# A gated cross-attention and mixture-of-experts kernel: where a bias is added to the residual rows, and in which order the last expert tile is multiplied

## The chip, the cores and the metric

The kernel runs on one core of a Trainium2 chip. Its engines are the TensorE (PE in the profile, its weight loads PEld), the VectorE (DVE), the ScalarE (ACT), the GpSimd (POOL) and the SyncE (SP), which only issues DMAs here. Each engine works through its own queue of instructions in a fixed order and meets the others at semaphores. The metric is device time in microseconds (us); lower is better. The kernel before took 1280.68 us (median of 3 runs, 1278.86 to 1280.71).

## What is computed

Two blocks, each with an attention part and a feed-forward part that is added to the residual x (4 batches of 512 rows, 512 columns, float32). The change lies wholly in the last part of the second block, a mixture of 8 experts (inner width 352) with 2 experts per row and a shared expert (inner width 704) for every row:

```python
probs = softmax(x @ router_w.T)
topk_w, topk_idx = top_k(probs, 2); topk_w /= sum(topk_w)
for each expert e:                       # weight ce per row, 0 for most rows
    acc += ce * (silu(x @ gate_w[e]) * (x @ up_w[e]) @ down_w[e])
shared = silu(x @ s_gate_w + s_gate_b) * (x @ s_up_w + s_up_b) @ s_down_w + s_down_b
x_out = x + tanh(g_ffn[1]) * (acc + shared)      # here "x @" means layernorm(x) @
```

## The kernel before

The 2048 rows are 16 tiles of 128 rows, 4 tiles to a batch. The residual lives in SBUF as `x_sb`, one 128x512 block per tile. The last part of the kernel is written as five stages.

**Norm and shared expert, first half (L1160 to L1303).** `normed(b)` takes the layer-norm statistics of the batch (DVE, L121/L122; then two small POOL instructions `ve` L124 and `rstd` L126) and, tile by tile, writes the normed rows to `vx` (DVE, L130), transposes them on the PE (`tpd`, L1170) and copies them to `xnT_d` (ACT, L1173). `shared_hidden(0, b, ...)` multiplies batch b by gate and up columns of the shared expert: three chunks, each 16 matmuls into one PSUM buffer `gu` (L1219), then silu with bias on ACT (`sg`, L1207) and the product on DVE (`hd`, L1208). The norm tiles of batch b+1 are laid between the chunks of batch b. `shared_down(b)` multiplies by the down weights (`od`, L1255) and a DVE instruction (L1262) adds the result to `x_sb`; it runs one batch behind. PSUM has three such large buffers (`big`), which `gu`, `tpd`, `gue` and `oe` share, and two smaller ones (`acc`).

**Routing (L1307 to L1408).** A chain of small DVE instructions picks the two experts per row, counts them (PE, L1346 and L1354), and works out for every row the slot in a list sorted by expert. It ends with the row numbers `goi` (L1404).

**Scattering (L1410 to L1420).** 32 indirect DMAs issued by POOL (L1413) write the normed rows to the list `slots` in DRAM.

**Bias and shared expert, second half (L1428 to L1439).** The shared expert's down bias, already multiplied by the gate (`sdb`, made by L1126 and L1127), is added to all 16 tiles of `x_sb` by 16 POOL instructions in L1429. Then come the remaining gate and up columns, the last `shared_down` and two calls of `shared_down_two`, which also write `x_sb` to the output.

**Experts (L1442 to L1537).** The list has up to 39 tiles of 128 slots (`MT`); 36 of them are worked through here, the last three stand in a branch on the number used and are not entered with these inputs. For each tile j: `slot_rows` loads the rows (`xr`) and, where the expert changes, its weights, and turns the rows on the PE (`tpe`); `slot_hidden` makes 16 matmuls `gue` (gate and up in turn for each quarter of the depth), silu (`sge`, ACT) and the product (`he`, DVE); `slot_turn` turns it (`tph_e` on PE, `hT` on DVE); `slot_down` makes 6 matmuls `oe`, copies them (`ye`, ACT), and POOL issues an indirect DMA (L1499) that adds the 128 rows to the output. These adding DMAs are chained by hand: each waits until the one before has landed. The loop in `slot_tiles` is staggered: tile j's `slot_hidden` comes before tile j-1's turn and down.

The order of each engine's queue is made at compile time. Program order is the priority, but an instruction whose inputs are expected ready earlier is put ahead of earlier-written ones that are expected to wait. So the queue is not the text: the 4 bias adds of batch 3 run at 716 us, long before the routing that is written ahead of them, while those of batches 0 to 2 follow the L1262 additions to the same rows, at 759, 792 and 827 us. `tc.keep_in_program_order(ins)` pins an instruction behind the one written before it on the same engine.

Of the kernel before, what the change touches and what calls it, by code (L numbers as in the profile page):

```python
# [10 lines left out]
F32 = mybir.dt.float32  # L11
# [4 lines left out]
AF = mybir.ActivationFunctionType  # L16
ALU = mybir.AluOpType
# [3 lines left out]
P = 128  # L21
B, S, D = 4, 512, 512
NT = B * S // P
TB = S // P
DC = D // P
# [4 lines left out]
E, I = 8, 352  # L30

ICH = ((0, 128), (128, 128), (256, 96))
# [16 lines left out]
def flamingo_kernel(  # L49
# [22 lines left out]
    nc = tc.nc  # L72
# [6 lines left out]
    def big(name):  # L79
        return ps_big.tile([P, 2, 512], F32, tag="big", name=name)  # L80
# [5 lines left out]
    ident = const.tile([P, P], F32, name="ident")  # L86
# [7 lines left out]
    x_sb = const.tile([P, NT, D], F32, name="x_sb")  # L94
# [20 lines left out]
    def layer_norm_stats(b, tag, add=nc.vector):  # L115

        t0 = b * TB
        mv = small.tile([P, TB, 2], F32, tag="mv", name=f"mv_{tag}_{t0}")
        for i in range(TB):
            st = small.tile([P, 6], F32, tag="st", name=f"st_{tag}_{t0 + i}")  # L120
            nc.vector.bn_stats(st, x_sb[:, t0 + i, :])  # L121
            nc.vector.bn_aggr(mv[:, i, :], st)  # L122
        ve = small.tile([P, TB], F32, tag="ve", name=f"ve_{tag}_{t0}")
        add.tensor_scalar_add(ve, mv[:, :, 1], LN_EPS)  # L124
        rstd = small.tile([P, TB], F32, tag="rstd", name=f"rstd_{tag}_{t0}")
        nc.gpsimd.tensor_tensor(rstd, ve, mhalf, ALU.pow)  # L126
        return mv, rstd
# [104 lines left out]
    state = {"pend": None}  # L232
# [227 lines left out]
    def given(t):  # L460
        b, i = divmod(t, TB)
        return [(lambda cols=WHOLE, g=g: project(b, i, g, cols)) for g in range(NG)]
# [18 lines left out]
    for n in range(last_n + 1):  # L481
# [12 lines left out]
        elif n >= 7:  # L494
            stand_sums(behind, n, 1, n - 3)
            o = given(n - 7)
# [620 lines left out]
    fpool = ctx.enter_context(tc.tile_pool(name="fpool", bufs=2))  # L1117
# [7 lines left out]
    sdb = dpool.tile([P, D], F32, name="sdb")  # L1125
# [34 lines left out]
    def normed(b):  # L1160

        state["d"] = layer_norm_stats(b, "d", nc.gpsimd)

        def one_tile(i):
            t = b * TB + i
            v = vx[:, t, :D]
            layer_norm(v, t, i, *state["d"])
            tp = big(f"tpd_{t}")
            for dc in range(DC):
                nc.tensor.transpose(  # L1170
                    tp[:, 0, dc * P : (dc + 1) * P], v[:, dc * P : (dc + 1) * P], ident
                )
            nc.scalar.copy(  # L1173
                xnT[:, :, t * P : (t + 1) * P], tp[:, 0, :].rearrange("p (c q) -> p c q", q=P)
            )

        return [lambda i=i: one_tile(i) for i in range(TB)]
# [34 lines left out]
    def shared_hidden(n, b, h, chunks, between=()):  # L1212
        gw, uw, _ = shared_w[n]
        between = list(between)
        for c in range(chunks):
            gu = big(f"gu_{n}_{b}_{c}")
            for m, w in enumerate((gw, uw)):
                for dc in range(DC):
                    nc.tensor.matmul(  # L1219
                        gu[:, m, :],  # L1220
                        lhsT=w[:, dc, c * P : (c + 1) * P],
                        rhs=xnT[:, dc, b * S : (b + 1) * S],
                        start=dc == 0,
                        stop=dc == DC - 1,
                    )
            gate_up(gu, n, c, h[:, c, :], f"{n}_{b}_{c}")
            while between and (c == chunks - 1 or len(between) >= TB - c):
                between.pop(0)()
# [69 lines left out]
    pend = None  # L1298
    for b in range(B):
        h = hidden_rows(f"hd_0_{b}")  # L1300
        shared_hidden(0, b, h, 3, normed(b + 1) if b + 1 < B else [routed] + 3 * [lambda: None])
        if pend is not None:
            shared_down(*pend)  # L1303
        pend = (b, h)
# [21 lines left out]
    for n in range(2):  # L1326
        m, f = rt(f"m{n}", 1), rt(f"f{n}", 1)
        h = rt(f"hot{n}")
# [16 lines left out]
    for k in range(NT):  # L1345
        nc.tensor.matmul(  # L1346
            pos[:, k * E :],
            lhsT=before if k == 0 else ones_h,
            rhs=flat[:, : (NT - k) * E],
            start=k == 0,  # L1350
            stop=k == NT - 1,
        )
    for t in range(NT):
        nc.tensor.matmul(  # L1354
            pos_ps[:, 1, :E],
            lhsT=ones_h,
            rhs=taken[:, t, :],
            start=t == 0,
            stop=t == NT - 1,
# [39 lines left out]
    for n in range(2):  # L1399
        w = rt(f"w{n}")  # L1400
# [24 lines left out]
        out=row_i, in_=slots[:, D:].rearrange("(j p) n -> p j n", p=P), allow_slow_non_contiguous=True  # L1425
    )

    for t in range(NT):  # L1428
        nc.gpsimd.tensor_tensor(x_sb[:, t, :], x_sb[:, t, :], sdb, ALU.add)  # L1429
    down = shared_down  # L1430
    for b in range(0, B, 2):
        h = [hidden_rows(f"hd_1_{b}")]
# [5 lines left out]
        down, pend = shared_down_two, (b, h)  # L1438
# [3 lines left out]
    def slot_rows(j):  # L1442
        xr = fpool.tile([P, D], F32, tag="xr", name=f"xr_{j}", bufs=3)
        nc.sync.dma_start(out=xr, in_=slots[j * P : (j + 1) * P, :D])
        e = nc.sync.value_load(of_i[0:1, j : j + 1], min_val=0, max_val=2 * E - 1)
        w = load_weights(
            e_w[bass.ds(e % E, 1), :, :].rearrange("e p f -> (e p) f"), (j + 2) % 3, cond=e < E
        )
        tp = acc(f"tpe_{j}")
        for dc in range(DC):  # L1450
            nc.tensor.transpose(
                tp[:, dc * P : (dc + 1) * P], xr[:, dc * P : (dc + 1) * P], ident
            )
        xT = fpool.tile([P, DC, P], F32, tag="xT", name=f"xT_{j}")
        nc.scalar.copy(xT, tp.rearrange("p (c q) -> p c q", q=P))
        return xT, w

    def slot_hidden(j, xT, w):
        gw, uw, dw = w
        gu = big(f"gue_{j}")  # L1460
        for dc in range(DC):
            for m, wt in enumerate((gw, uw)):
                nc.tensor.matmul(  # L1463
                    gu[:, m, :I],
                    lhsT=xT[:, dc, :],
                    rhs=wt[:, dc, :],
                    start=dc == 0,
                    stop=dc == DC - 1,
                )
        sg = fpool.tile([P, I], F32, tag="sge", name=f"sge_{j}", bufs=1)  # L1470
        nc.scalar.activation(sg, gu[:, 0, :I], AF.Silu)  # L1471
        h = fpool.tile([P, I], F32, tag="he", name=f"he_{j}", bufs=1)
        nc.vector.scalar_tensor_tensor(
            h, gu[:, 1, :I], row_i[:, j, 1:2], sg, ALU.mult, ALU.mult
        )
        return h, dw

    def slot_turn(j, h, dw):
        tp = acc(f"tph_e_{j}")
        for c, (i0, ni) in enumerate(ICH):  # L1480
            nc.tensor.transpose(tp[:ni, c * P : (c + 1) * P], h[:, i0 : i0 + ni], ident)  # L1481
        hT = fpool.tile([P, len(ICH), P], F32, tag="hT", name=f"hT_{j}")
        nc.vector.tensor_copy(hT[:, :2, :], tp[:, : 2 * P].rearrange("p (c q) -> p c q", q=P))  # L1483
        nc.vector.tensor_copy(hT[:96, 2, :], tp[:96, 2 * P : 3 * P])
        return hT

    def slot_down(j, hT, dw):
        o_ps = big(f"oe_{j}")
        for c, (_, ni) in enumerate(ICH):
            nc.tensor.matmul(  # L1490
                o_ps[:, 0, :],
                lhsT=hT[:ni, c, :],
                rhs=dw[:ni, c, :],
                start=c == 0,
                stop=c == len(ICH) - 1,
            )
        y = fpool.tile([P, D], F32, tag="row", name=f"ye_{j}", bufs=5)
        nc.scalar.copy(y, o_ps[:, 0, :])  # L1498
        added = nc.gpsimd.indirect_dma_start(  # L1499
            out=out,  # L1500
            out_offset=bass.IndirectOffsetOnAxis(ap=row_i[:, j, 0:1].bitcast(I32), axis=0),
            in_=y,
            in_offset=None,
            bounds_check=B * S + P - 1,
            oob_is_err=True,
            compute_op=ALU.add,
        )

        if adds:
            tc.add_manual_dep(  # L1510
                added.ins,
                adds[-1].ins.name,
                mybir.DependencyInfo(mybir.DependencyClass.Sync, mybir.DependencyReason.DATA),
                reason="rows added in turn",
            )
        adds.append(added)

    def slot_tiles(j0, j1):
        adds.clear()
        rows = slot_rows(j0)  # L1520
        pend = None
        for j in range(j0, j1):
            got = slot_hidden(j, *rows)
            if pend is not None:
                hT = slot_turn(j - 1, *pend)
            if j + 1 < j1:
                rows = slot_rows(j + 1)
            if pend is not None:
                slot_down(j - 1, hT, *pend[1:])
            pend = got  # L1530
        slot_down(j1 - 1, slot_turn(j1 - 1, *pend), *pend[1:])

    adds = []
    slot_tiles(0, MT - 3)
    with tc.If(used > MT - 3):
        slot_tiles(MT - 3, MT)
# [76 lines left out]
```

## Time and profile before

| | us |
|---|---|
| median of 3 runs | 1280.68 |
| the profiled execution | 1278.66 |
| its span in the trace | 1277.0 |
| PE busy | 1169.5 (92% of the span) |
| DVE busy | 607.1 |
| ACT busy | 510.9 |
| POOL busy | 410.9 |

What lies around the span in the profiled execution is 1.66 us (1278.66 less 1277.0). The page's fifth part lists groups of like instructions with their busy time; its fourth part is the chain of work that ended last. For the stages here the timeline is of more use: one line per instruction or run of like instructions, with start, length, engine, line of the code, output and inputs, and in brackets how long the engine had been idle before it and what ended the idle time.

| stretch, us | what | PE busy, us | granted PE clock |
|---|---|---|---|
| 710 to 770 | norm, shared expert first half | 59.32 of 60 | 1.00 |
| 770 to 840 | the same, routing | 70.00 of 70 | 1.00 |
| 840 to 890 | scattering, second half begins | 44.50 of 50 | 0.93 |
| 890 to 960 | second half of the shared expert | 69.96 of 70 | 1.00 |
| 970 to 1240 | experts | 267.43 of 270 | 1.00 |
| 1240 to 1252 | experts | 11.84 of 12 | 1.00 |
| 1252 to 1277 | last tile and end | 11.08 of 25 | 0.79 |

### The profile page before, as it was taken

To read this page: it belongs to the slowest core of one execution; us is meant where nothing else is said; L and a number is where in the kernel's file an instruction comes from. 1 tells how busy PE (TensorE), PEld (TensorE's weight loads), DVE (VectorE), ACT (ScalarE), POOL (GpSimd) and SP (SyncE) were. 2 spreads that over 40 slices of the span, in tenths; PEclk is the share of its full clock that TensorE was granted. 3 is DMA by queue.
4 is the path that set the end of the run, shared out by engine and by line. 5 is a ranking of instruction groups with operands and counts; after the bars stand their busy time and mean duration, and the time that the engine had idled before them with its cause. 6 is when DMAs were issued, how large, how long until landed. Compare 5 with 4: busy or idle time off the path is not lost. (4 is left out here: it accounts for less than half of the span.)

```text
span 1277.0 us, 14308 instructions
## 1 busy us (share of the span) xinstructions
PE 1169.5 (92%) x5246; PEld 531.7 (42%) x5262; DVE 607.1 (48%) x1157; ACT 510.9 (40%) x710; POOL 410.9 (32%) x409
## 2 busy tenths in 40 slices
PE   3777897899899999999999999998999999999995
PEld 1333443344233333333333444443335555555553
DVE  7699999788557666656554511321221111111110
ACT  4688898686355554544454211100001112121121
POOL 1000100111277777767776311155000111111111
PEclk8878899999899999999999999998999999999998
DMA  9230232335021211211003000066116786888782
GB/s 342 72 131 12 42 62 42 85 79 118 28 68 34 67 35 35 67 34 59 2 1 141 9 1 1 0 230 183 62 63 189 231 266 187 262 262 253 202 247 34
DMA packets 88752, 135.32 MB, mean 106 GB/s; under 512 B 52836, under 2 KB 54120, under 8 KB 84840
## 3 DMA queue, kind: packets, MB, share of 16 engines
q1 hardware_dynamic: 80936, 116.52, 28.9%
q0 software_dynamic: 7744, 17.86, 6.6%
q8 instruction: 42, 0.69, 0.2%
q14 instruction: 30, 0.25, 0.1%
HBM read 113.84 MB, written 32.32 MB: 114 GB/s over the span
## 5 line engine op out<-in xcount | busy, mean ns | idle before, releaser
L428 ACT ACTIVATE ex<-s,mbias,mk 128x1024 f32<-128x1024 f32 x128 | 147.2, 1200 | 143.3 <-PE s L239 143.3
L319 DVE TENSOR_REDUCE nmax<-s 128x2 f32<-128x1024 f32 x128 | 150.3, 1215 | 100.4 <-PE s L239 89.6
L1463 PE MATMUL gue<-w,xT 128*128 128x352 f32 x576 | 176.1, 459 | 0.0
L1499 POOL DMA_INDIRECT out_dram<-ye,row_i x36 | 55.5, 1541 | 327.5 <-ACT ye L1498 230.1
L389 POOL TENSOR_TENSOR part<-part,ex 128x1024 f32<-128x1024 f32 x62 | 144.6, 2352 | 16.5 <-PE sm L239 11.4
L1219 PE MATMUL gu<-xnT_d,w 128*128 128x512 f32 x320 | 140.4, 593 | 0.7 <-ACT xnT_d L1173 0.7
L1463 PEld LDWEIGHTS gue<-w,xT 128*128 128x128 f32 x576 | 109.2, 190 | 70.6 <-issue 16.9
L1483 DVE COPY hT<-tph_e 128x256 f32<-128x256 f32 x36 | 15.3, 425 | 255.2 <-PE tph_e L1481 255.2
L1490 PE MATMUL oe<-w,hT 128*128 128x512 f32 (+1 forms) x216 | 102.4, 609 | 3.8 <-ACT ye L1498 0.6
L1219 PEld LDWEIGHTS gu<-xnT_d,w 128*128 128x128 f32 x320 | 59.9, 190 | 73.9 <-issue 72.1
L761 PE MATMUL oa<-ctx,vTa 128*128 128x512 f32 x128 | 69.5, 694 | 18.8 <-ACT vTa L758 18.7
L1207 ACT ACTIVATE sg<-gu,sgb 128x512 f32<-128x512 f32 x20 | 13.7, 687 | 175.9 <-PE gu L1219 154.0
L389 POOL TENSOR_TENSOR part<-ex,ex 128x1024 f32<-128x1024 f32 x32 | 75.8, 2388 | 24.1 <-ACT ex L428 24.1
L1471 ACT ACTIVATE sge<-gue 128x352 f32<-128x352 f32 x36 | 16.8, 465 | 151.5 <-PE gue L1463 151.5
L239 PE MATMUL s<-row_tables 10*128 10x512 bf16 (+1 forms) x512 | 67.7, 387 | 9.3 <-DVE nmax L319 5.9
L239 PE MATMUL s<-k,qT 32*128 32x512 f32 x512 | 72.8, 610 | 0.4 <-ACT qT L287 0.4
L239 PE MATMUL s<-qT,k 32*128 32x512 f32 x512 | 71.8, 601 | 0.0
L239 PE MATMUL av<-ex,kv 128*32 128x512 f32 x512 | 70.1, 612 | 0.4 <-ACT ex L428 0.4
L239 PE MATMUL q_ps<-xnT,wq_sb 128*128 128x512 f32 (+1 forms) x156 | 69.4, 557 | 0.0
L912 PE MATMUL ob<-w2q,hqT 128*128 128x512 bf16 x248 | 58.8, 381 | 11.3 <-DVE hqT L838 10.4
L1208 DVE SCALAR_TENSOR_TENSOR hd<-gu,sub,sg 128x512 f32<-128x512 f32 x20 | 15.0, 750 | 111.7 <-ACT sg L1207 98.8
L239 PE MATMUL oc<-wo,attnT 128*128 128x512 f32 (+1 forms) x164 | 66.2, 525 | 0.0
(261 smaller groups left out, 1648.6 us busy)
## 6 DMA issues: line engine op xcount, KB each, us to landing
w<-in_e_w_dram SPq DMA_DIRECT2D x36, 1408.0 KB
w<-in_e_w_dram SPq DMA_DIRECT2D x36, 768.0 KB
slots<-row_tables SPq DMA_DIRECT2D x13, 771.0 KB
xr<-slots SPq DMA_DIRECT2D x36, 256.0 KB
stage<-in_w1T_dram SPq DMA_DIRECT2D x4, 1024.0 KB
stage<-in_w2T_dram SPq DMA_DIRECT2D x4, 1024.0 KB
k<-kv SPq DMA_DIRECT2D x64, 64.0 KB
out_dram<-x_sb SPq DMA_DIRECT2D x16, 256.0 KB
```

The lines of the kernel that those rows point to most:

```text
L239: tc.keep_in_program_order(nc.tensor.matmul(*args, **how))
L319: largest = nc.vector.tensor_reduce(nmax[:, i, 2 * j : 2 * j + 2], sc[j], AX.X, ALU.max, negate=True)
L389: nc.gpsimd.tensor_tensor(part[:, hs, :], old[:, hs, :], ex[:, hs, :], ALU.add)
L428: nc.scalar.activation(ex[:, 2 * j : 2 * j + 2, :], sc[j], AF.Exp, bias=mbias[:, b, kc : kc + 1], scale=mk[:, b, kc : kc + 1],)
L761: nc.tensor.matmul(o_ps[:, 0, :], lhsT=vT[:, dc, :], rhs=cq[:, dc, :], start=dc == 0, stop=dc == DC - 1,)
L912: nc.tensor.matmul(o_ps, lhsT=hqT[:, c, :], rhs=w2q[:, c * D : (c + 1) * D], start=c == 0, stop=c == IC - 1,)
L1219: nc.tensor.matmul(gu[:, m, :], lhsT=w[:, dc, c * P : (c + 1) * P], rhs=xnT[:, dc, b * S : (b + 1) * S], start=dc == 0, stop=dc == DC - 1,)
L1463: nc.tensor.matmul(gu[:, m, :I], lhsT=xT[:, dc, :], rhs=wt[:, dc, :], start=dc == 0, stop=dc == DC - 1,)
L1471: nc.scalar.activation(sg, gu[:, 0, :I], AF.Silu)
L1483: nc.vector.tensor_copy(hT[:, :2, :], tp[:, : 2 * P].rearrange("p (c q) -> p c q", q=P))
L1490: nc.tensor.matmul(o_ps[:, 0, :], lhsT=hT[:ni, c, :], rhs=dw[:ni, c, :], start=c == 0, stop=c == len(ICH) - 1,)
L1499: added = nc.gpsimd.indirect_dma_start(out=out, out_offset=bass.IndirectOffsetOnAxis(ap=row_i[:, j, 0:1].bitcast(I32), axis=0), in_=y, in_ ...
```

## The change

Two parts, independent of each other.

The first moves the bias adds. The loop of 16 POOL instructions between scattering and second half is gone; in its place each batch's four adds stand in the loop over batches, after `shared_hidden(0, b, ...)` and ahead of the down projection of the batch before. For every batch they are now written before the `shared_down` that adds to the same rows.

```diff
     for b in range(B):
         h = hidden_rows(f"hd_0_{b}")
         shared_hidden(0, b, h, 3, normed(b + 1) if b + 1 < B else [routed] + 3 * [lambda: None])
+        for t in range(b * TB, (b + 1) * TB):
+            nc.gpsimd.tensor_tensor(x_sb[:, t, :], x_sb[:, t, :], sdb, ALU.add)
         if pend is not None:
             shared_down(*pend)
...
-    for t in range(NT):
-        nc.gpsimd.tensor_tensor(x_sb[:, t, :], x_sb[:, t, :], sdb, ALU.add)
```

The second concerns the last tile of `slot_tiles`. The tile before it (34 here) is turned first; then the last tile's (35) gate matmuls run, all four quarters of the depth; then tile 34's `slot_down`; then tile 35's up matmuls; then tile 35's turn and down. The PE instructions of this stretch are pinned to program order. The silu of tile 35 is written right behind the gate matmuls. The tiles before keep their order.

```diff
-    def slot_hidden(j, xT, w):
+    def slot_hidden(j, xT, w, between=None):
...
+        fix = (lambda ins: None) if between is None else tc.keep_in_program_order
+        sg = fpool.tile([P, I], F32, tag="sge", name=f"sge_{j}", bufs=1)
+        order = [(dc, m) for dc in range(DC) for m in range(2)]
+        if between is not None:
+            order.sort(key=lambda o: o[1])
+        for dc, m in order:
+            if between is not None and (dc, m) == (0, 1):
+                nc.scalar.activation(sg, gu[:, 0, :I], AF.Silu)
+                between()
...
-        for j in range(j0, j1):
+        for j in range(j0, j1 - 1):
             got = slot_hidden(j, *rows)
             if pend is not None:
                 hT = slot_turn(j - 1, *pend)
-            if j + 1 < j1:
-                rows = slot_rows(j + 1)
+            rows = slot_rows(j + 1)
             if pend is not None:
                 slot_down(j - 1, hT, *pend[1:])
             pend = got
-        slot_down(j1 - 1, slot_turn(j1 - 1, *pend), *pend[1:])
+
+        j = j1 - 1
+        state["fix"] = tc.keep_in_program_order
+        hT = slot_turn(j - 1, *pend)
+        got = slot_hidden(j, *rows, lambda: slot_down(j - 1, hT, *pend[1:]))
+        slot_down(j, slot_turn(j, *got), *got[1:])
+        state["fix"] = lambda ins: None
```

In `slot_turn` and `slot_down` every PE instruction is passed through `state["fix"]`, which pins it in that stretch and does nothing elsewhere.

More of the change, by code (lines that the diff above doesn't have):

```diff
@@ L1456, in slot_rows @@
         return xT, w
-    def slot_hidden(j, xT, w):
+    def slot_hidden(j, xT, w, between=None):
         gw, uw, dw = w
         gu = big(f"gue_{j}")
-        for dc in range(DC):
-            for m, wt in enumerate((gw, uw)):
+        fix = (lambda ins: None) if between is None else tc.keep_in_program_order
[7 more added lines that the diff above has]
+                between()
+            wt = (gw, uw)[m]
+            fix(
                 nc.tensor.matmul(
@@ L1469, in slot_hidden @@
                 )
-        sg = fpool.tile([P, I], F32, tag="sge", name=f"sge_{j}", bufs=1)
-        nc.scalar.activation(sg, gu[:, 0, :I], AF.Silu)
+            )
+        if between is None:
+            nc.scalar.activation(sg, gu[:, 0, :I], AF.Silu)
         h = fpool.tile([P, I], F32, tag="he", name=f"he_{j}", bufs=1)
@@ L1480, in slot_turn @@
         for c, (i0, ni) in enumerate(ICH):
-            nc.tensor.transpose(tp[:ni, c * P : (c + 1) * P], h[:, i0 : i0 + ni], ident)
+            state["fix"](
+                nc.tensor.transpose(tp[:ni, c * P : (c + 1) * P], h[:, i0 : i0 + ni], ident)
+            )
         hT = fpool.tile([P, len(ICH), P], F32, tag="hT", name=f"hT_{j}")
@@ L1489, in slot_down @@
         for c, (_, ni) in enumerate(ICH):
[L1490 to L1495, printed above, removed]
+            state["fix"](
+                nc.tensor.matmul(
+                    o_ps[:, 0, :],
+                    lhsT=hT[:ni, c, :],
+                    rhs=dw[:ni, c, :],
+                    start=c == 0,
+                    stop=c == len(ICH) - 1,
+                )
             )
@@ L1530, in slot_tiles @@
             pend = got
-        slot_down(j1 - 1, slot_turn(j1 - 1, *pend), *pend[1:])
+        j = j1 - 1
[4 more added lines that the diff above has]
+        state["fix"] = lambda ins: None
     adds = []
+    state["fix"] = lambda ins: None
     slot_tiles(0, MT - 3)
```

## The prediction

> **What bounds the kernel now.** The page's first part gives the PE 92% of the span, and the table of stretches says where the other 8% of this stage lies: 5.5 us in 840 to 890 and 14 us after 1252. Elsewhere from 710 on the PE hardly waits, so only three things can change the time: those two places, and a new stall of the PE. I read the end first, in the timeline.
>
> ```profile
> 1256.80 0.46 ACT L1471 ACTIVATE sge<-gue 128x352 f32<-128x352 f32 x1 [4.15 <-PE gue L1463]
> 1257.61 2.84 PE L1490 MATMUL oe<-w,hT 128*128 128x512 f32 x6 [0.52 <-DVE hT L1483]
> 1260.29 0.49 PE L1481 MATMUL tph_e<-ident,he 128*128 128x128 f32 x3
> 1260.49 0.58 ACT L1498 COPY ye<-oe 128x512 f32<-128x512 f32 x1 [3.23 <-PE oe L1490]
> 1261.35 1.54 POOL L1499 DMA_INDIRECT out_dram<-ye,row_i  x1 [6.88 <-ACT ye L1498]
> 1264.20 0.58 ACT L1498 COPY ye<-oe 128x512 f32<-128x512 f32 x1 [3.12 <-PE oe L1490]
> 1267.91 1.54 POOL L1499 DMA_INDIRECT out_dram<-ye,row_i  x1 [5.02 <-DMA out_dram<-ye,row_i]
> ```
>
> The last add waits not for its own rows (`ye` of tile 35 is done at 1264.78) but for tile 34's add to land. The chain of waits puts that landing at 1267.19 (5.80 us after its issue) and has 0.5 to 0.7 us from each landing to the next issue. From the last issue to the end of the span it is 9.1 us, which the change doesn't touch.
>
> Then the stall at 840 to 890, in the timelines of ACT and PE and the table of 2 us stretches (columns: busy PE, PEld, DVE, ACT, POOL; clock; DMA share; GB/s).
>
> ```profile
> 864.45 0.69 ACT L1207 ACTIVATE sg_h<-gu_h,sgb 128x512 f32<-128x512 f32 x1 [14.90 <-remote]
> 866.63 7.33 PE L1255 MATMUL od<-w,hd 128*128 128x512 f32 x12 [5.50 <-DVE x_sb L1262]
> 862.00:864.00 2.00, 0.00 (x0) 0.00 (x0) 0.00 (x0) 0.00 (x0) 0.40 (x1) 0.92 0.78 271
> 864.00:866.00 2.00, 0.00 (x0) 0.00 (x0) 0.83 (x2) 0.69 (x1) 0.23 (x1) 0.50 0.03 8
> ```
>
> `gu_h` is done near 855.8, yet ACT starts its silu only at 864.45. DVE's product and two L1262 additions stand behind it, and the PE behind those. "Remote" is a releaser that the trace doesn't see; the last packets of the first 16 scatters pass between 864.0 and 864.5, so I read it as something of ACT's (probably its own code) that comes in only when that backlog is gone.
>
> **Part one, what it removes.** The start of the scatters hangs on the routing chain:
>
> ```profile
> 834.86 1.26 POOL L1429 TENSOR_TENSOR x_sb<-x_sb,sdb 128x512 f32<-128x512 f32 x1 [1.31 <-DVE x_sb L1262]
> 835.17 0.98 DVE L1365 CAST n_i<-n_f 128x8 int32<-128x8 f32 x1
> 836.38 0.17 DVE L1368 CAST n_f<-n_i 128x8 f32<-128x8 int32 x1
> 841.36 1.26 POOL L1413 DMA_INDIRECT slots<-vx,goi  x1 [5.24 <-DVE goi L1404]
> ```
>
> Two casts of the same 1024 elements take 0.98 and 0.17 us. The long one ends at 836.15, and the bias add beside it at 836.12: the cast waited for the add. With that add gone from here the chain is 0.98 - 0.17 = 0.81 us shorter, and scatters and first weight load start as much sooner. What it is worth at the PE isn't shown: nothing, if ACT's release stands at a time of its own; 0.81, if it follows the draining of the scatters, whose 16 issues keep their 1.27 us pace. A loss would need the backlog to be longer, and its bytes are the same. I take 0.8, since release and drain coincide to 0.5 us. From 866.63 to 960 the PE is busy throughout, so what is gained there arrives at the experts.
>
> **Part one, what it adds.** All 16 adds can now start when `sdb` is scaled (DVE, ends at 709.70) and their rows are normed, so on POOL they fill about 710 to 733. Nothing waits for them soon: the first L1262 is at 758.54. But they stand ahead of other POOL work, batch 3's `ve` and `rstd` (714.25 to 715.61), of which the adds of batches 0 and 1 are written first; and they run beside eight DVE norms of batches 1 and 2, which now take 3.73 us from 709.61. How that goes the trace shows at 716:
>
> ```profile
> 715.64 1.01 DVE L130 TENSOR_SCALAR vx<-x_sb,mv_d,rstd_d 128x512 f32<-128x512 f32 x2 [1.48 <-POOL rstd_d L126]
> 715.64 3.83 DVE L130 TENSOR_SCALAR vx<-x_sb,mv_d,rstd_d 128x512 f32<-128x512 f32 x4 [1.48 <-POOL rstd_d L126]
> 716.27 5.55 POOL L1429 TENSOR_TENSOR x_sb<-x_sb,sdb 128x512 f32<-128x512 f32 x4 [0.66 <-DVE vx L130]
> 719.38 0.74 DVE L1208 SCALAR_TENSOR_TENSOR hd<-gu,sub,sg 128x512 f32<-128x512 f32 x1
> 724.95 0.60 PE L1170 MATMUL tpd<-ident,vx 128*128 128x128 f32 x4
> ```
>
> Two norms without adds take 1.01 us, the two beside them 3.83 - 1.01 = 2.82, some 1.4 each; the adds themselves take 5.55 / 4 = 1.39. The two engines take turns at about 1.5 us for a pair (the row's longest norm is 1.494). By this row seven of the eight norms (the first is under way) end at 710.1 + 7 x 1.5 = 720.6 instead of 713.3; the last statistics (0.90) bring 721.5, and the first `hd`, if next in DVE's queue, ends at 722.3.
>
> The Trainium skill has a rule that speaks against the change here: "SBUF — State Buffer", in its summary rules for authors, says that GpSimd and a VectorE instruction in a two-port mode hold their shared port alone for a whole instruction, so the second to issue is fully blocked. By it each norm waits a whole add, 1.26 + 0.54 (median norm) = 1.8 us: 710.1 + 7 x 1.8 = 722.7, and `hd` ends at 724.4. What decides is the PE: there are three large PSUM buffers, `gu` of the first chunk holds one until that `hd`, and the PE wants it for the transposes at 724.95. Before, `hd` ends at 720.13, a slack of 4.8 us. By row 2.7 us of it are left, by rule 0.5; either way **cost 0**, if `hd` is not queued behind more.
>
> The L1262 additions now wait for adds done 25 us before: nothing. The 12 adds gone from 759 to 836 freed POOL, which was idle there anyway. SP's queue is untouched except for starting with the routing result.
>
> **Part two.** Times follow the steady pace of the tiles. `oe` of tile 33 starts at 1249.18 and takes 2.68 to the next PE work (1251.86); he_34 is ready at 1249.62, so the turn of tile 34 goes there with no wait and takes 0.33 of the PE (as from `tph_e` to `tpe`, 1248.17 to 1248.50). Gate, 8 of the 16 `gue` at 0.289: from 1252.2, 2.31, and some 0.1 to the next kind: 1254.6. hT_34 is ready near 1253.0 (1.0 after its turn), so `oe` of tile 34 runs at once, 1254.6 to 1257.3. Its `ye` starts 2.88 after `oe` (1249.18 to 1252.06): 1257.5, and its add 0.86 later: 1258.4. Tile 33's add landed at 1257.78; with 0.72 from landing to issue that is 1258.5, which decides. So tile 34's add is issued at **1258.5 instead of 1261.35**.
>
> Up runs from 1257.3; its product `he` starts at 1257.3 + 2.31 + 0.32 = 1259.9 (the 0.32 as from 16 x 0.289 to 4.94 before). This `he` (0.58) now stands in the open: the turn starts at 1260.6, against 1260.29 before. From turn to `oe` 1.0, to `ye` 2.85, to the issue 0.86: own rows ready at **1265.3**. Tile 34's add lands at 1258.5 + 5.80 = 1264.3, plus 0.72 is 1265.0. The later is 1265.3: the last wait is now that of the tile's own rows, by 0.3, and the gain is 1267.91 - 1265.3 = **2.6 us**. No instruction is added, and ACT keeps its order (silu of 35, then `ye` of 34). The pinning costs nothing unless a pinned instruction is late; in the worked times none is but the turn of tile 35.
>
> **Sum.** 1278.66 - 0.8 - 2.6 = 1275.3 us for the profiled execution. That execution was 2.0 us under the median of the runs; for the median I take 1280.68 - 3.4 = **1277.3**. Own range 1275.2 to 1278.4 (a gain of 2.3 to 3.5, the upper end from the median, the lower from the profiled execution). About 0.2% (2.6 us) is what a measurement of this kernel can tell from no change, so this forecast is just outside.
>
> **Rivals.**
> - *The norms of batch 3 block the first `hd` (slower).* Before, batch 3's four norms stand in DVE's queue ahead of that `hd` (715.64, then 719.38). If the queue keeps this order and `rstd` stands behind the eight adds of batches 0 and 1, then: adds 709.8 + 8 x 1.5 = 721.8; `ve` and `rstd` 1.36: 723.2; four norms beside the next adds, 0.5 + 3 x 1.5: 728.2; `hd` 0.75: 729.0. The PE stands from 724.95, 4.1 us. It decides from 4.8 us of delay on. To that comes the clock: the rows above show 0.50 after some 2.6 us of idling (0.92 as the mean of 862 to 864 is half clock from 863.7 on; the PE stopped at 861.1), and the 12 `od` behind it took 7.33, where 12 took 5.42 at 855.72: 1.9 us more. The skill's "TensorE: Matmul & The Clock Gate", Part 1, has half clock after an idle window of some 3.4 us that runs free, so by the rule a 4.1 us stall may or may not pay this; by the row it does, and I take the row. 4.1 + 1.9 - 3.4 = +2.6: 1281.3 here, **1283.3** as median. Against: the queue is made anew, and if `rstd` is expected late, `hd` goes first. The trace can't say which. Chance 0.27.
> - *Only one part arrives.* ACT's release doesn't follow the scatters: -2.6, 1278.1. Or tile 34's add lands later: the chain of waits has adds beside weight loads of up to 9.52 us (1085.65), which gives 1258.5 + 9.5 + 0.7 = 1268.7, 0.8 later than before, and nothing in all: 1280.7. Against the latter: no weight load is issued after 1244, and the adds at 1244.50 and 1252.92 landed in 4.56 and 4.86. Chance 0.17 together.
> - *Queues reordered in a way I don't see*, such as a PE order of the shared stage that exposes a wait: +1 to +6. Chance 0.08.
>
> **Chances.** The forecast has 0.48. Faster by over 0.2%: most of that and a sliver of the second rival, 0.47. Within: its lower edge, the rest of the second rival, and the milder half of the slow case, 0.24. Slower: the harsher half of the slow case, a little of it by noise, and the last, 0.29. The range reaches over the slow case.
>
> **What would show it.** In the changed trace: L1365's cast at about 0.17 and the first scatter near 840.5; ACT's `sg_h` near 863.7; norms of 1.4 to 1.5 us beside adds from 709.8; no PE gap at 725; `oe` of tile 34 between two runs of 8 `gue`; the two last adds 6.8 us apart, the last released by `ye` and not by a DMA. A PE gap behind 724 with `hd` as its end proves the first rival; last adds 8 us or more apart prove the second.

## The result, and the profile after

| | before | after |
|---|---|---|
| median, us | 1280.7 (4 runs, 1278.86 to 1281.24) | 1286.14 (4 runs, 1285.01 to 1287.54) |
| profiled execution, us | 1278.66 | 1286.71 |
| its span, us | 1277.0 | 1285.0 |
| PE busy, us | 1169.5 | 1171.8 |

The changed kernel is slower: ratio 1.0053, 95% interval 1.0040 to 1.0066. The forecast was 1277.3, its own range ended at 1278.4, and its slow case stood at 1283.3: the time lies above all three.

The page's fifth part names the place, here before and after. The columns are line, engine, operation and count, then busy time and mean ns, then the idle time just before the group and what ended it.

```profile
L1219 PE MATMUL gu<-xnT_d,w 128*128 128x512 f32 x320 | 140.4, 593 | 0.7 <-ACT xnT_d L1173 0.7
L1219 PE MATMUL gu<-xnT_d,w 128*128 128x512 f32 x320 | 143.2, 603 | 7.0 <-DVE hd L1208 6.3
```

The group has gained 6.3 us of waiting for `hd` and 2.8 us of busy time, with the same 320 matmuls. The PE's timeline shows both in one chunk (first line: before; the others: after):

```profile
725.39 7.03 PE L1219 MATMUL gu<-xnT_d,w 128*128 128x512 f32 x16
...
726.37 0.60 PE L1170 MATMUL tpd<-ident,vx 128*128 128x128 f32 x4
733.28 9.89 PE L1219 MATMUL gu<-xnT_d,w 128*128 128x512 f32 x16 [6.31 <-DVE hd L1208]
```

To set the two executions side by side, take the PE's first `tpd` of this stage: 707.46 before, 708.87 after. These 1.41 us are not the change's; nothing ahead of that point is touched, and over the executions of this study the first `tpd` lies anywhere from 706.10 to 710.52. The chunk above began at 725.39 before, so it should begin at 726.80 and is 6.48 late; and it takes 9.89 instead of 7.03. That is 9.34 us, and the next row confirms it (744.91 against 734.16: 10.75, less 1.41).

Why `hd` is late is read from DVE's timeline, and why DVE was late from POOL's. Before, the eight norms of batches 1 and 2 and batch 3's `rstd` were:

```profile
709.61 3.73 DVE L130 TENSOR_SCALAR vx<-x_sb,mv_d,rstd_d 128x512 f32<-128x512 f32 x8
```

```profile
714.57 1.04 POOL L126 TENSOR_TENSOR rstd_d<-ve_d,mhalf 128x4 f32<-128x4 f32 x1
```

After, DVE and POOL:

```profile
711.10 10.41 DVE L130 TENSOR_SCALAR vx<-x_sb,mv_d,rstd_d 128x512 f32<-128x512 f32 x8
...
728.75 3.81 DVE L130 TENSOR_SCALAR vx<-x_sb,mv_d,rstd_d 128x512 f32<-128x512 f32 x4 [6.43 <-POOL rstd_d L126]
732.48 1.40 DVE L1208 SCALAR_TENSOR_TENSOR hd<-gu,sub,sg 128x512 f32<-128x512 f32 x2
```

```profile
711.27 15.03 POOL L1303 TENSOR_TENSOR x_sb<-x_sb,sdb 128x512 f32<-128x512 f32 x11 [1.05 <-DVE sdb L1127]
726.27 0.23 POOL L124 TENSOR_SCALAR ve_d<-mv_d 128x4 f32<-128x4 f32 x1
726.46 1.27 POOL L1303 TENSOR_TENSOR x_sb<-x_sb,sdb 128x512 f32<-128x512 f32 x1
727.68 1.03 POOL L126 TENSOR_TENSOR rstd_d<-ve_d,mhalf 128x4 f32<-128x4 f32 x1
```

Eleven adds stand on POOL ahead of batch 3's `ve`, and a twelfth between `ve` and `rstd`. On DVE the four norms of batch 3 still stand ahead of the first `hd`, as they did before. So `hd` waits for norms it has nothing to do with, those wait for `rstd`, and `rstd` waits for twelve adds that nobody needs for another 30 us. The statistics of batch 3 had been ready since 722.32 (L122, 722.14 and 0.18 long).

The longer chunk is the clock. In the table of stretches (columns as before: busy PE, PEld, DVE, ACT, POOL; granted clock; DMA share; GB/s):

```profile
729.00:731.00 2.00, 0.00 (x0) 0.00 (x0) 2.00 (x3) 0.00 (x0) 1.62 (x2) 1.00 0.00 0
731.00:733.00 2.00, 0.00 (x0) 0.00 (x0) 2.00 (x3) 0.00 (x0) 2.00 (x2) 0.76 0.00 0
733.00:735.00 2.00, 1.72 (x2) 0.84 (x3) 0.88 (x2) 0.00 (x0) 1.91 (x2) 0.50 0.00 0
...
737.00:739.00 2.00, 2.00 (x4) 0.86 (x3) 0.00 (x0) 0.00 (x0) 0.00 (x0) 0.53 0.00 0
739.00:741.00 2.00, 2.00 (x6) 0.90 (x5) 0.00 (x0) 0.00 (x0) 0.00 (x0) 1.00 0.00 0
```

The clock falls to half 1.2 us before the PE goes on (732.04 against 733.28), and comes back only at 739.

At the scattering stage the cast no longer waits for an add (it took 0.98 before), and ACT's release, the gap and the matmuls behind it look like this, in the timelines of DVE, ACT and PE:

```profile
845.92 0.17 DVE L1367 CAST n_i<-n_f 128x8 int32<-128x8 f32 x1
```

```profile
874.42 0.69 ACT L1207 ACTIVATE sg_h<-gu_h,sgb 128x512 f32<-128x512 f32 x1 [14.11 <-remote]
```

```profile
876.60 8.19 PE L1255 MATMUL od<-w,hd 128*128 128x512 f32 x12 [4.72 <-DVE x_sb L1262]
```

The gap is 0.78 shorter (5.50 before), but the twelve `od` take 8.19 instead of 7.33: nothing is left of the gain in this execution.

The tail does what it was meant to do. PE and POOL:

```profile
1262.96 2.53 PE L1473 MATMUL gue<-w,xT 128*128 128x352 f32 x8
1265.33 2.74 PE L1504 MATMUL oe<-w,hT 128*128 128x512 f32 x6
1267.91 2.53 PE L1473 MATMUL gue<-w,xT 128*128 128x352 f32 x8
1271.19 0.55 PE L1493 MATMUL tph_e<-ident,he 128*128 128x128 f32 x3 [0.75 <-DVE he L1484]
```

```profile
1269.28 1.54 POOL L1514 DMA_INDIRECT out_dram<-ye,row_i  x1 [4.05 <-ACT ye L1513]
1275.99 1.54 POOL L1514 DMA_INDIRECT out_dram<-ye,row_i  x1 [5.17 <-ACT ye L1513]
```

`oe` of tile 34 lies between the gate and up of tile 35, and the last add is released by its own rows, not by a DMA. From the end of the late `od` (873.96 before, 884.79 after) to the last add it is 393.95 before and 391.20 after: 2.75 gained.

The sum for the profiled execution: 1.41 (start) + 9.34 (stall and clock) + 0.08 (scattering: 884.79 - 873.96 = 10.83, less 10.75) - 2.75 (tail) = 8.08, against 8.0 between the spans.

### The profile page after: what moved, and what is told of

Same layout as the page of the kernel before. It is cut to its first block, busy times and chain, and to the rows that moved or that the text cites. A ratio compares the mean times of both kernels' runs of the same rounds, so it can differ in the third digit from the quotient of the medians.

```text
span 1285.0 us, 14299 instructions
## 1 busy us (share of the span) xinstructions
PE 1171.8 (91%) x5246; PEld 532.3 (41%) x5262; DVE 613.0 (48%) x1157; ACT 511.3 (40%) x710; POOL 411.8 (32%) x409
## 5 line engine op out<-in xcount | busy, mean ns | idle before, releaser
L1219 PE MATMUL gu<-xnT_d,w 128*128 128x512 f32 x320 | 143.2, 603 | 7.0 <-DVE hd L1208 6.3
L912 PE MATMUL ob<-w2q,hqT 128*128 128x512 bf16 x248 | 64.2, 407 | 14.0 <-DVE hqT L838 10.3
```

The costliest lines, as they stand in the source:

```text
L912: nc.tensor.matmul(o_ps, lhsT=hqT[:, c, :], rhs=w2q[:, c * D : (c + 1) * D], start=c == 0, stop=c == IC - 1,)
L1219: nc.tensor.matmul(gu[:, m, :], lhsT=w[:, dc, c * P : (c + 1) * P], rhs=xnT[:, dc, b * S : (b + 1) * S], start=dc == 0, stop=dc == DC - 1,)
```

## The experiments

Theory: part one loses 9 us at 725, because `hd` stands on DVE behind norms that wait on POOL behind the moved adds; part two gains its 2.7 us untouched. Rivals: the two parts disturb each other; or the adds are slow in themselves (DVE and POOL taking turns) rather than badly placed. The ratios are to runs of the kernel before on the same chip. The runs came in four groups, each on one chip: e1, e2, e3 and e5 (before: 1280.28); e4 and e6 (1280.37); e7 and e8 (1272.25); the four of the last paragraph (1272.28).

**The parts alone.** Both are edits of the changed kernel. e1 puts the adds back where they were and keeps the tail:

```diff
-        for t in range(b * TB, (b + 1) * TB):
-            nc.gpsimd.tensor_tensor(x_sb[:, t, :], x_sb[:, t, :], sdb, ALU.add)
...
+    for t in range(NT):
+        nc.gpsimd.tensor_tensor(x_sb[:, t, :], x_sb[:, t, :], sdb, ALU.add)
```

e2 takes the tail back, all of it, and keeps the moved adds (two places are shown):

```diff
-        for j in range(j0, j1 - 1):
+        for j in range(j0, j1):
...
+        slot_down(j1 - 1, slot_turn(j1 - 1, *pend), *pend[1:])
```

> The last tile's new order alone, the bias adds where they were. Theory (the loss is all from the bias adds, the new order of the last tile gains what was worked out): 2.6 to 2.8 us under the kernel before, 1278.0 at a median of 1280.7, no PE gap at 725, last two adds 6.7 us apart. Rival (the pinned order or the earlier silu costs time elsewhere): at or above the kernel before.

> The bias adds moved alone, the last tile as before. Theory: the PE stall of 6.3 us and 2.9 us of half clock near 727 to 743 return, the cast is 0.17 us and the scatters start 0.8 us earlier against the PE, so 8.4 to 9.3 us over the kernel before, near 1289.5; with e1 the two differences add up to that of the changed kernel. Rival (the parts act on each other): they don't add up.

e1: 1277.28 us, ratio 0.9982 (0.9974 to 0.9990), no gap at 725, last adds 6.74 apart. e2: 1288.63 us, ratio 1.0071 (1.0059 to 1.0084), with the gap (its profiled execution, 1284.54, was the fastest of six). The same chunk in e1 and in e2:

```profile
724.97 7.03 PE L1219 MATMUL gu<-xnT_d,w 128*128 128x512 f32 x16
...
730.63 8.77 PE L1219 MATMUL gu<-xnT_d,w 128*128 128x512 f32 x16 [6.44 <-DVE hd L1208]
```

The two differences add up to +0.0053, the ratio of the whole change; within the intervals the parts don't disturb each other, and all of the loss is part one's.

**`hd` ahead of the norms.** e3 leaves all 16 adds early and changes one thing in DVE's queue: batch 3's norms are put behind the first `hd` (`state["mixed"]`, filled by a line that is not shown, lists the `hd` in program order: 0 to 2 are batch 0's).

```diff
-            layer_norm(v, t, i, *state["d"])
+            with tc.issue_after(state["mixed"][0]) if b == B - 1 else nullcontext():
+                layer_norm(v, t, i, *state["d"])
```

> The changed kernel with one edge more in the VectorE's queue: batch 3's four norms stand behind the first product hd, all adds stay early and beside the norms. Theory (queue order is the cause): hd ends near 724 by the changed kernel's own times (last statistics end at 722.3, plus 0.75), before the PE wants the buffer at 726.4; the stall of 6.3 us goes, a rest of under 1 us may stand at the next wait for a buffer near 733; 1277.3 to 1279, below the kernel before. Rival (the shared port alone makes the VectorE late, whatever the order): the stall stays at 3 us or more, 1283 or more.

Measured 1276.89 us, ratio 0.9974 (0.9963 to 0.9985). DVE's timeline of e3:

```profile
711.12 10.41 DVE L130 TENSOR_SCALAR vx<-x_sb,mv_d,rstd_d 128x512 f32<-128x512 f32 x8
...
722.53 0.75 DVE L1209 SCALAR_TENSOR_TENSOR hd<-gu,sub,sg 128x512 f32<-128x512 f32 x1 [0.19 <-issue]
728.78 3.82 DVE L130 TENSOR_SCALAR vx<-x_sb,mv_d,rstd_d 128x512 f32<-128x512 f32 x4 [5.50 <-POOL rstd_d L126]
```

The norms are as slow as in the changed kernel and start as late, behind `rstd`, yet the PE has no gap: `hd` is done at 723.28, 3.5 us before its buffer is wanted (the PE starts that `gu` at 726.80). So the slow adds and norms cost nothing once `hd` is ahead of them. This is also the case that the forecast assumed, and it came out at the forecast's ratio (1277.3 to 1280.68 is 0.9974), in part by luck: the scattering stage gave less than forecast and the tail a little more.

**Fewer adds early.** e5 holds the adds of batch b until `hd` number b, so that none runs ahead of `rstd`; e4 does so for batches 2 and 3 alone and leaves eight adds ahead, the number that the slower rival had counted. The edit of e4 (e5 is the same without the line `if b > 1`):

```diff
-            nc.gpsimd.tensor_tensor(x_sb[:, t, :], x_sb[:, t, :], sdb, ALU.add)
+            added = nc.gpsimd.tensor_tensor(x_sb[:, t, :], x_sb[:, t, :], sdb, ALU.add)
+            if b > 1:
+                tc.add_manual_dep(
+                    added.ins,
+                    state["mixed"][b].name,
+                    mybir.DependencyInfo(mybir.DependencyClass.Sync, mybir.DependencyReason.DATA),
+                    reason="behind the norms",
+                )
```

> The changed kernel with the adds of batch b waiting for the VectorE's product hd number b (first one near 720), so that no add runs beside a norm and none stands ahead of batch 3's rstd. Theory: norms at 0.54 us, no stall at 725, cast at 0.17 us, scatters 0.8 us earlier, last tile as changed: 2.6 to 3.4 us under the kernel before, 1277.3 to 1278.1, the fastest. Rival (ScalarE's wait at 849 to 864 doesn't follow the scatters): its end doesn't move and only 2.6 us are gained.

> As e5, but only batches 2 and 3 wait for their hd; the 8 adds of batches 0 and 1 stay early, ahead of batch 3's rstd and beside the norms. Theory (the first hd is late by the adds ahead of rstd, each some 1.4 us, on top of the norms' 1.3 to 1.5): eight norms again in some 10.4 us, but rstd starts behind 8 adds and not 12, near 14.5 us after the first tpd instead of 18.8, the last four norms run alone in 1.9, and hd ends about 18 us after the first tpd, when the PE wants the buffer (17.9 to 18.1): a PE gap of 0 to 0.5 us and no half clock; time as e5 within 0.5 us. Rival (any norm beside an add makes the stall): a gap of 3 us or more and 1281 or more.

e5: 1276.88 us, ratio 0.9972 (0.9960 to 0.9983), norms back at 3.74 us for eight. e4: 1276.49 us, ratio 0.9968 (0.9955 to 0.9981). In e4 the queue has the bad order and still there is no stall; POOL and DVE:

```profile
711.52 11.35 POOL L1304 TENSOR_TENSOR x_sb<-x_sb,sdb 128x512 f32<-128x512 f32 x8 [1.18 <-DVE sdb L1127]
...
723.15 1.03 POOL L126 TENSOR_TENSOR rstd_d<-ve_d,mhalf 128x4 f32<-128x4 f32 x1
```

```profile
724.21 1.92 DVE L130 TENSOR_SCALAR vx<-x_sb,mv_d,rstd_d 128x512 f32<-128x512 f32 x4 [1.65 <-POOL rstd_d L126]
726.05 0.74 DVE L1208 SCALAR_TENSOR_TENSOR hd<-gu,sub,sg 128x512 f32<-128x512 f32 x1
```

`hd` ends at 726.79, and the PE wants the buffer when the transposes at 726.48 are through, at 726.92. With eight adds ahead the slack is just used up. In the changed kernel four more stand there, and batch 3's own adds, which e4 holds back, slow the four norms from 1.92 to 3.81 us. So the bad order alone doesn't make the loss; it takes the order and more adds than these eight. e3, e4 and e5 all beat both kernels and can't be told from each other.

**What holds ACT at `sg_h`.** In every execution above, before and after, the PE also idles for 4.5 to 5.5 us in the scattering stage, because ACT starts `sg_h` late, by a releaser called "remote". The release came 22.9 to 23.1 us after the first scatter in seven traces (before, after, e1 to e5), which speaks for the scatters; against that, what `sg_h` reads comes from no scatter. If it is code of ACT's that has to be fetched at a fixed place of its queue, 8 more instructions ahead should move it (e6). If it is the scatters, holding them back should (e7). All start from e5. The copies of e6 (8, and 64 of them in e8) run at about 790 us:

```diff
+        if b == 2:
+            for k in range(8):
+                tc.keep_in_program_order(nc.scalar.copy(tiny[:, k : k + 1], mhalf[:, 0:1]))
```

In e7 the first 16 scatters wait for the `hd` of the half chunk (`behind`):

```diff
+                if n == 0:
+                    tc.add_manual_dep(
+                        sent.ins,
+                        behind.name,
+                        mybir.DependencyInfo(
+                            mybir.DependencyClass.Sync, mybir.DependencyReason.DATA
+                        ),
+                        reason="behind the half chunk",
+                    )
```

> e5 with eight small ScalarE copies (128x1, into a spare tile) put into the ScalarE's queue behind batch 2's work, near 790, where it is idle. Theory A (ScalarE's wait at 849 to 864, which ends 23.0 us after the first scatter in all kernels so far, is for its own code, fetched behind the scatters): the place of the fetch moves eight instructions forward, to before the scatters, the wait of 14 us goes, the PE gap of 4.5 us and the half clock of some 2.4 us behind it go, about 1270. Theory B (it waits for something of the scatters themselves): nothing moves, 1276.9 as e5.

> e5 with the first 16 scatters held until the VectorE's product of the half chunk (the hd behind sg_h) is done, some 15 us later than before. Theory (what holds sg_h for 14 us is the backlog of the scatters, and these aren't needed until the experts at 958): sg_h starts right behind gu_h near 856 to 859, the PE gap of 4.5 us and its half clock go, 1276.9 less 5 to 7 = 1270 to 1272, if the same wait doesn't fall on a later silu that the PE needs. Rival (sg_h is held by the weight loads that start at 840, or by nothing of the DMAs): sg_h starts as late as before and the scatters behind it, no gain or a loss.

> As e6 with 64 small ScalarE copies instead of 8. If the wait of sg_h were for the ScalarE's code, a shift of 64 instructions would move it away even where 8 didn't; by what e6 showed it stays, ending 23.0 us after the first scatter, at about the time of e5.

e6: 1276.35 us, ratio 0.9972 (0.9961 to 0.9983). The wait is where it was, 22.90 us after the first scatter (842.95):

```profile
865.85 0.69 ACT L1207 ACTIVATE sg_h<-gu_h,sgb 128x512 f32<-128x512 f32 x1 [13.89 <-remote]
```

e7: 1269.74 us, ratio 0.9976 (0.9968 to 0.9984); e8: 1267.98 us in one run. Neither shows the wait. But on that chip the kernel before took 1272.25, 8 us less than on the others, so its own wait had to be looked at before either could count. Hence the last four: the kernel before unchanged, and e5, e7 and e8 again.

> The kernel before once more, unchanged, to see on this chip whether ACT's release of sg_h waits at all. Theory (the wait belongs to the program): TensorE idles 5.5 us before the twelve od of the scattering stage, and sg_h ends its wait about 23 us after the first scatter began. Rival (the wait belongs to the chip or to the execution): no idle time over 1 us there.

> The adds behind the hd products, as in e5_adds_behind_hd. Theory: idle time of 4.5 us before od, sg_h 23 us after the first scatter; time 0.9972 of before. Rival: no idle time when before has none either, and the ratio is the same, since both lose the wait.

> The same with the first sixteen scatters held back until the hd of the half chunk. If it is the scatters that hold sg_h, the wait (present in the two runs ahead) is gone here or stands 23 us after the later first scatter; the time is 4.5 + 2 us below e5_again, ratio about 0.992. If the scatters are only neighbours, the wait stands where it stood, 4.5 us, and the ratio is 0.997.

> The adds behind hd, and 64 small copies on ACT beforehand. If the wait is tied to the count of ACT's instructions, it moves to another place of ACT's queue or is gone, and 4.5 us of idle TensorE time go with it; if it is tied to the scatters it stands at sg_h, 23 us after the first of them.

This chip too took 1272.28 for the kernel before, and the unchanged kernel shows no wait there. ACT and PE of b_again:

```profile
856.90 0.69 ACT L1207 ACTIVATE sg_h<-gu_h,sgb 128x512 f32<-128x512 f32 x1 [6.34 <-PE gu_h L1237]
```

```profile
856.72 10.57 PE L1255 MATMUL od<-w,hd 128*128 128x512 f32 x24
```

The 24 `od` run in one piece. e5_again 0.9980 (0.9973 to 0.9987), e7_again 0.9981 (0.9971 to 0.9991) and e8_again 0.9981 (0.9974 to 0.9989) have no wait either. So whether ACT waits there goes with the chip (or with the time of its use, since each chip served one group only) and not with these kernels, and e7 and e8, which met only chips without the wait, say nothing of its cause.

What "remote" is stays open. e6 speaks against a fixed place in ACT's queue, as far as 8 instructions can. So do the packets that the trace lists as instructions: in the eight traces with the wait none arrives in the 13 us before the release (the kernel before has one between 850 and 851 and the next between 865 and 866, behind the start of `sg_h` at 864.45). The weight loads that start with the scatters are no better: in the kernel before their last packets ahead of the release pass between 855 and 856. And the backlog of the scatters does not do it alone: in b_again it lasts just as long, into 865 to 866, 23 us after the first scatter (842.37), and ACT doesn't wait. Where there is a wait, its tie to the scatters is a coincidence in time that no run has tested.

## Why the prediction was wrong

**The step that failed** is the one that costs the early adds: "**cost 0**, if `hd` is not queued behind more". The condition didn't hold. The text had it in the trace (the norms at 715.64 ahead of the `hd` at 719.38) and set it aside with "the queue is made anew, and if `rstd` is expected late, `hd` goes first". DVE's queue was not made differently: nothing on DVE was edited here, and its order of norms and `hd` came out as before. The mechanism was thus named, as the first rival, and given 0.27; e3 shows that with all adds early this order alone parts 0.9974 from 1.0053, and the PE stood 6.3 us where 0 was forecast.

**The rival's size was off too**, 4.1 + 1.9 against 6.5 + 2.9.
- Adds ahead of `rstd`: eight counted, because those of batches 0 and 1 are written first. Twelve stood there. Batch 2's adds are written behind batch 3's norm, but their rows are normed by then while `ve` still waits for DVE's statistics; that fits the planner's rule in the section on the kernel. With eight, the stall is nil in e4; with batch 3's adds beside the norms as well (3.81 - 1.92 = 1.89, less the 0.13 that e4 has left) it would be some 1.8, an estimate, and not 4.1.
- The pace: 1.5 per pair was the longest norm of the row at 716. Norm and add did take turns, one and one, but a pair took 1.41 (10.41 less the 0.54 of the first norm, over seven), because the records of neighbours overlap (the median norm's is 1.49 long). For the same reason the 1.8 that the prediction made of the rule in "SBUF — State Buffer", summary of rules for authors, by adding up two whole lengths, is too much; that one of the two waits for the other is what the turns show. In e3 `hd` ends at 723.28, which is 721.87 on the scale of before; the row's sum said 722.3, the rule's 724.4.
- The slack: the PE wanted the buffer for `gu` (725.39), not for the transposes at 724.95, which ran in time. 0.4 us more slack than taken.
- The clock: 1.9 was the `od` row's price, and this stall paid 2.86. The last section says why.

**What was right.** The cast fell to 0.17. ACT's release came at 874.42, which less 10.75 is 863.67; 863.7 was forecast. The chain behind this (release follows the scatters by a constant distance) held wherever the wait exists. But its worth, 0.8, was too high even there: counted from the first `tpd`, the late `od` end after 166.50 (before) and 166.46 us (e1) where the adds still lie behind the scattering, and after 165.99, 166.02, 166.01 and 166.06 where they don't (e3, e4, e5, e6). That is 0.46 us. They start 0.9 sooner, and the half clock takes back half. On a chip without the wait it is worth nothing: from the first `tpd` to the end of the 24 `od` it is 158.82 in b_again and 158.83 in e5_again.

The tail came out to a tenth. On the scale of before (less 10.77, by tile 34's `gue`) tile 34's add is issued at 1258.51 (forecast 1258.5), the turn of tile 35 starts at 1260.42 (1260.6), and the last add is issued at 1265.22 (1265.3). The gain was 2.75 where 2.6 had been worked out, and the same from the late `od` on in e3, e4 and e5 (391.20, 391.18 and 391.19 us to the last add, 391.26 in e1). The second rival, a late landing of tile 34's add, is ruled out by the release by `ye` in all of them.

## What to carry over

When work is moved to an engine with time to spare, list what stands behind it in that engine's queue, and follow each of those to the engine that the kernel is bound by: here `rstd`, 1 us long, behind twelve adds held four norms, these held one product, and that held the PE. Unless something shows otherwise, take it that the queue of an engine the edit doesn't touch keeps its order, as DVE's did here, and count the moved instructions by when their inputs are ready, not by where they are written. Slack hides a delay until it is used up: eight adds ahead, with batch 3's held back, were free; twelve, with batch 3's behind them, cost 9 us.

## What the hardware showed beyond that

In these stalls the half clock came in pieces of one length. From stretches of 1 us (of 0.5 and 0.2 us for the third row; a share of 0.74 in one of 1 us means half clock for 0.52 of it), start and end can be worked out. At half clock half of the work is lost, so half of what is left of the half clock when the PE goes on (sixth column) should be what the matmuls take longer (seventh):

| stall | PE idle from | half clock from, to | length | PE goes on | half clock left, halved | matmuls took longer by |
|---|---|---|---|---|---|---|
| after, 727 | 726.97 | 732.04, 738.86 | 6.82 | 733.28 | 2.79 | 2.86 |
| e2, 724 | 724.19 | 727.12, 733.96 | 6.84 | 730.63 | 1.67 | 1.74 |
| after, 872 | 871.88 | 875.39, 882.22 | 6.82 | 876.60 | 2.81 | 2.77 |
| before, 861 | 861.13 | 863.70, 870.52 | 6.82 | 866.63 | 1.95 | 1.91 |
| e5, 864 | 864.19 | 866.74, 873.58 | 6.84 | 868.73 | 2.43 | 2.38 |

The stalls of the scattering stage in e1, e2, e3, e4 and e6 give 6.82 to 6.84 as well. It is not the length of every piece: earlier parts of the kernel before have half clock for 3.41 us (635.00 to 638.41) and for 10.24 us (64.98 to 75.22). But 3.41, 6.83 and 10.24 are one, two and three times 3.413, and so is the full clock between 638.41 and 863.69 (225.28, 66 times). The clock changes on a grid of 3.413 us that keeps its beat over hundreds of microseconds.

With the table this says when it changes. Before, at 861, the PE was busy for 0.85 us of the piece of the grid that ends at 863.69, a quarter of it, and the clock fell there. After, at 727, it was busy for 1.76 us of the piece that ends at 728.62, and the clock fell only at the end of the next, wholly idle one. It came back at the end of the first piece that was busy throughout or nearly so (3.32 of 3.41 us in e2; in the changed kernel 2.17 of 3.41, from 733.28 on, were not enough). "TensorE: Matmul & The Clock Gate", Part 1, has such windows of some 3.4 us that run free of the kernel, and half clock after an idle one; the length agrees, but a window that is idle for three quarters was enough here.

Two things follow. The fall came between 2.6 and 5.1 us after the PE stopped, by where the stall lay on the grid; two stalls of like length (6.3 and 6.4) paid 2.86 and 1.74. And within such a piece, a stall that ends 1 us sooner is worth only 0.5: the PE has 1 us more to work in, but works in it at half speed. That is where half of the scattering stage's gain went.

The other surprise is the chip. The kernel before takes 1280.3 us on two chips and 1272.3 on two others, and by the traces of before and b_again nearly all of the difference lies in one place: 5.50 us of idle PE behind `sg_h` and the 1.91 us of half clock after it make 7.4 of the 8.0.
